# Moving the latents' transposes and the values' part of a folding from the experts' stage into attention's first unit

## The chip, the cores and the metric

The kernel runs on one core of one Trainium2 chip. The metric is the time of one execution on the device in microseconds (us); the time before is 1996.56 us, the median of three runs.

## What is computed

The reference is two layers of a transformer trunk on float32 tokens x of shape (4, 512, 512). Layer 0 adds a test-time-training attention and a ternary feed-forward network. Layer 1, with which the change deals, adds to x a latent attention and a mixture of four experts, both of the normalised x:

```
c_kv = xn @ W_DKV + b_DKV                         # 128 latent numbers per token
c_q  = xn @ W_DQ + b_DQ                           # 384
k, q = (c_kv @ W_UK + b_UK), (c_q @ W_UQ + b_UQ)  # 16 heads of 128
v    = c_kv @ W_UV + b_UV
q, k : first 64 numbers of each head replaced by rope(q @ W_QR), rope(k @ W_KR)
ctx  = softmax(q k^T / sqrt(128)) @ v             # per batch and head, 512 x 512 scores
x    = x + (ctx @ W_O + b_O) + experts(xn)
experts: token t goes to expert t % 4; silu(gate) * up, then down
```

## The kernel before

The program is one list of instructions for five engines: TensorE (PE; its weight loads are PEld), VectorE (DVE), ScalarE (ACT), GpSimd (POOL) and SyncE (SP). Every engine takes its own list in order and waits at an instruction until all that it needs is there; DMAs that SP or POOL issue stand in the same lists. A scheduler orders the lists, but instructions wrapped in `pin(...)` keep the order in which the program emits them. A tile with `bufs=1` has a single buffer: a load into it waits until the readers of its last content are done.

Layer 0 comes first and ends with the latents in memory. Two stages of layer 1 follow.

**The experts' stage** (about 1000 to 1136 us). For each expert e, `hidden(e)` computes four blocks of the gated hidden layer (products `epg` and `epu`, line L976, 128x256 each; copies `hold` on ACT, L1008 to L1014), and `returned` the way back (`epo`, L1039; for the last two experts `eox` and `eo`, L1069). Into this stage small work for attention is mixed:

- `fold` for head group 0. There are 16 heads in four head groups of four heads. Folding multiplies the up-projections of a head group by the rope's matrices (`pw`, L866: four 128x64 products each, for `uk` and three `uq`), and the values' up-projection by the rows of W_O (`pvo`, L891: one 128x512 product per head; the copy to `vo` on ACT, L892), so that attention's output comes from latents directly. `fold` is a generator; each `next` moves it one stage on: it loads a block `raw` (L883), transposes it on DVE into `wt` (L877), and multiplies. The values' part is the fifth block. It also loads one head's 128 rows of W_O into `ow` (L857), once per head, and DVE adds these rows, scaled by a bias, to `bo_part` (L895, L897). In this stage `ow` has two buffers and is loaded from SP's queue.
- for each of the four batches, four PE transposes of the latents `ckv` (`lv_tr`, L1157), and one copy on ACT to `lv` (L1158).

**The attention stage** (1136 us to the end) runs 16 units, one per head group and batch, head group outermost. A unit has four steps i, one for each 128 query rows. A step emits: the scores of four heads (`sc`, L1207, twelve products into four banks), the softmax in five slices (DVE: maximum L1225, reciprocal L1231, transpose `tt` L1236; ACT: exponential L1227, scaling L1232; then 16 DMAs `prT` on SP, L1246), between the slices a quarter of the next unit's up-projections (`pk` and `pq`, L1184; rope on DVE L1191 and L1194 and on POOL L1195, other parts on ACT L1198), one slice of the previous unit's output product (`px`, `p`, L1301), one `next` of the next head group's folding, and the context product of two steps before (`pc`, L1254, four products with `lv`; copied to `ctxT`, L1256). For each head group POOL makes four sums and differences of `vo` into `t_ops` (L1274 to L1277), which the output products read. The first unit has no output product, and its steps 0 and 1 have no context product.

In this stage `fold` is called with one buffer for `ow`, loaded from POOL's queue. Its end for each head is:

```
            pv = psum(f"pvo_{hg}_{h}")
            pin(nc.tensor.matmul(pv, lhsT=wt[:, h, :], rhs=ows[h], start=True, stop=True))
            pin(nc.scalar.copy(w["vo"][:, h, :], pv))
            ...
            if h + ow_bufs < HPG:
                output_rows(h + ow_bufs)
            if h % 2 or ow_bufs == 1:
                yield
```

and the order at the end of a step is:

```
                advance(1, outs)
                advance(1, soft)
                advance(1, folds)
                if n > 1:
                    context_of(n - 2)
```

The folding of head group hg+1 begins with the first unit of head group hg.

## Time and profile before

| | |
|---|---|
| runs | 1996.56 us median of 3 (1992.72, 1996.56, 1998.15) |
| the profiled execution's own time | 1996.04 us |
| its span in the profile | 1994.3 us |
| mean granted clock of PE | 0.994 |
| PE busy | 1938.3 us, 97% |
| DVE, ACT, POOL busy | 1169.6, 816.1, 528.2 us |
| experts' last hidden layer | 1081.6 to about 1112 us |
| attention's first unit, steps 0 to 3 | 1149.4 to 1192 us |

Times in views are us from the span's start. A float32 product is two records of PE in the timeline (twelve score products are 24 records), a PE transpose one; the end of a record is modelled, so the cost of a group is best read from its start to the start of the next. Idle time in square brackets stands in front of the instruction, with what ended it.

### The profile page before, as it was taken

How to read it: one execution, taken by the hardware profiler on the slowest of the kernel's cores; microseconds unless marked ns; L12 is line 12 of the kernel's file. 1: busy time of each engine (PE TensorE's matmuls, PEld its weight loads, DVE VectorE, ACT ScalarE, POOL GpSimd, SP SyncE). 2: the span in 40 equal slices, each digit the busy share in tenths (PEclk: the TensorE clock that was granted, in tenths of full speed). 3: DMA queues.
4: the chain of work that ended last, by engine and by line, in shares of the span. 5: the costliest groups of instructions: out<-in, count | busy, mean ns of one | idle time of the engine just before them, and what ended most of it. 6: DMA issues, size and time to landing. Idle time of an engine off the chain costs nothing.

```text
span 1994.3 us, 32414 instructions
## 1 busy us (share of the span) xinstructions
PE 1938.3 (97%) x11626; PEld 1233.3 (62%) x11626; DVE 1169.6 (59%) x2579; ACT 816.1 (41%) x1695; POOL 528.2 (26%) x643
## 2 busy tenths in 40 slices
PE   8999999999999999998999999999999999999999
PEld 6777676767766676753777744555555555555555
DVE  4445748466666657474555656556555655655565
ACT  2234333334433443422222155455545545555552
POOL 5333343424333342512000101111211121222223
PEclk9999999999999999999999999999999999999999
DMA  6757566646456455745651135444344444333344
GB/s 170 210 130 209 143 185 167 175 120 179 141 145 189 126 173 159 224 128 195 225 168 49 58 94 141 118 106 104 101 111 108 103 110 108 95 101 98 89 115 117
DMA packets 226924, 273.51 MB, mean 137 GB/s; under 512 B 88587, under 2 KB 117452, under 8 KB 226124
## 3 DMA queue, kind: packets, MB, share of 16 engines
q1 hardware_dynamic: 204928, 237.19, 43.3%
q0 software_dynamic: 9760, 28.41, 5.0%
q10 hardware_dynamic: 12076, 5.84, 1.0%
q8 instruction: 93, 1.52, 0.3%
q14 instruction: 67, 0.55, 0.1%
HBM read 174.18 MB, written 34.87 MB: 105 GB/s over the span
## 4 chain that ended last, share of the span: by engine, by line
PE 49%; DVE 1%; DMA 0%; ACT 0%; issue 0%; SPq 0%; DVEq 0%; ACTq 0%
PE pc L1254 11%; PE sc L1207 9%; PE pq L1184 8%; PE px L1301 5%; PE p L1301 4%; PE pk L1184 3%; PE epg L976 3%; PE epo L1039 1%; PE epu L976 1%; PE eox L1069 1%; PE pvo L891 1%; PE pw L866 1%; PE eo L1069 1%; DMA gu<-in_gu 0%; DVE st L1225 0%; ACT prob L1227 0%
## 5 line engine op out<-in xcount | busy, mean ns | idle before, releaser
L1225 DVE TENSOR_REDUCE st<-sc 128x1 f32<-128x512 f32 x256 | 168.9, 681 | 244.0 <-PE sc L1207 244.0
L1227 ACT ACTIVATE prob<-sc,st 128x512 f32<-128x512 f32 x256 | 175.1, 686 | 210.5 <-DVE st L1225 210.3
L1254 PE MATMUL pc<-prT,lv 128*128 128x512 f32 x512 | 230.8, 593 | 0.0
L1232 ACT ACTIVATE prob<-prob,st 128x512 f32<-128x512 f32 x256 | 181.9, 720 | 58.8 <-DVE st L1231 58.8
L1236 DVE STREAM_TRANSPOSE tt<-prob 128x512 f32<-128x512 f32 x256 | 178.4, 700 | 43.0 <-ACT prob L1232 36.5
L117 PE MATMUL pf<-xT,wg 128*128 128x256 f32 x704 | 175.6, 391 | 6.2 <-DMA wg<-in_wg 4.4
L1184 PE MATMUL pq<-cq,uq 128*128 128x512 f32 x384 | 175.2, 592 | 0.0
L117 PE MATMUL pf<-xT,wu 128*128 128x256 f32 x704 | 167.6, 381 | 1.5 <-DMA wu<-in_wu 1.5
L117 PE MATMUL pd<-wd,hid 128*128 128x512 f32 x352 | 166.1, 600 | 1.3 <-DMA wd<-in_wd 1.2
L1254 PEld LDWEIGHTS pc<-prT,lv 128*128 128x128 f32 x512 | 96.4, 190 | 100.1 <-issue 98.1
L117 PEld LDWEIGHTS pf<-xT,wg 128*128 128x128 f32 x704 | 133.2, 194 | 33.5 <-issue 4.7
L1207 PE MATMUL sc<-k,q 32*128 32x512 f32 x1024 | 145.7, 617 | 2.5 <-ACT prob L1227 2.5
L117 PEld LDWEIGHTS pf<-xT,wu 128*128 128x128 f32 x704 | 134.5, 191 | 20.5 <-DMA wu<-in_wu 1.9
L478 DVE SCALAR_TENSOR_TENSOR hid<-pf,us,sg 128x256 f32<-128x256 f32 x88 | 42.0, 478 | 156.9 <-ACT sg L477 156.4
L1184 PEld LDWEIGHTS pq<-cq,uq 128*128 128x128 f32 x384 | 74.1, 193 | 90.7 <-issue 90.0
L314 POOL TENSOR_SCALAR sk<-k,m 128x256 f32<-128x256 f32 x64 | 61.2, 968 | 179.9 <-PE pz L117 167.7
L1195 POOL TENSOR_TENSOR kr<-kr,t2k 128x512 f32<-128x512 f32 x16 | 20.3, 1270 | 332.3 <-DVE t2k L1194 332.3
L421 POOL TENSOR_SCALAR gh<-grad,m 128x256 f32<-128x256 f32 x64 | 61.2, 966 | 154.5 <-DVE grad L390 131.6
L117 PEld LDWEIGHTS pd<-wd,hid 128*128 128x128 f32 x352 | 63.4, 190 | 60.2 <-issue 43.8
L1207 PEld LDWEIGHTS sc<-k,q 32*128 32x128 f32 x1024 | 48.4, 185 | 82.7 <-issue 73.2
L477 ACT ACTIVATE sg<-pf,gs 128x256 f32<-128x256 f32 x88 | 41.6, 473 | 132.8 <-PE pf L117 132.3
L1256 ACT COPY ctxT<-pc 128x512 f32<-128x512 f32 x64 | 37.4, 585 | 127.2 <-PE pc L1254 127.1
(316 smaller groups left out, 3467.9 us busy)
## 6 DMA issues: line engine op xcount, KB each, us to landing
prT<-tt SPq DMA_DIRECT2D x992, 64.0 KB, 2.0
wd<-in_wd SPq DMA_DIRECT2D x176, 256.0 KB, 3.1
wg<-in_wg SPq DMA_DIRECT2D x88, 256.0 KB, 3.0
wu<-in_wu SPq DMA_DIRECT2D x88, 256.0 KB, 3.1
cq<-lat_d SPq DMA_DIRECT2D x48, 256.0 KB, 3.8
rows<-rows SPq DMA_DIRECT2D x128, 66.0 KB, 2.2
kv<-rows POOLq DMA_DIRECT2D x32, 264.0 KB, 4.1
gu<-in_gu SPq DMA_DIRECT2D x3, 2048.0 KB
```

The costliest lines, as they stand in the source:

```text
L117: nc.tensor.matmul(out, lhsT=lhsT, rhs=rhs, start=start, stop=stop, skip_group_check=True)
L314: nc.gpsimd.tensor_scalar_mul(sk[:, :, :, h, :], at(k1[ch], slice(0, P)), m2[:, h : h + 1])
L421: nc.gpsimd.tensor_scalar_mul(gh[:, :, h, :], g, m2[:, h : h + 1])
L976: nc.tensor.matmul(ps, lhsT=w[:, c, :], rhs=x[:, c], start=start and c == 0, stop=c == 1, skip_group_check=True)
L1184: nc.tensor.matmul(ps, lhsT=columns(ws[hg][w]), rhs=x, start=(i == 0), stop=(i == len(srcs) - 1))
L1207: nc.tensor.matmul(ps[h], lhsT=qk[f"q{c}"][r, i * P : (i + 1) * P], rhs=qk[f"k{c}"][r, :], start=(n == 0), stop=(n == 2),)
L1225: pin(nc.vector.tensor_reduce(mx, ps[h], AX.X, ALU.max, negate=True))
L1227: pin(nc.scalar.activation(pr, ps[h], AF.Exp, bias=mx, scale=1.0, accum_out=sm))
L1232: pin(nc.scalar.mul(pr, pr, sm))
L1236: nc.vector.transpose(out=tt[:, :, h - 2], in_=pr.rearrange("p (k kq j) -> p kq k j", kq=4, j=32))
L1254: pin(nc.tensor.matmul(pc, lhsT=lv[:, b, k, :], rhs=at[:, :, k, :], start=(k == 0), stop=(k == E - 1)))
L1301: nc.tensor.matmul(ps[:, q, :], lhsT=a[:, k, q * P : (q + 1) * P], rhs=w[:, k, :], start=start and k == 0 and q == 0, stop=k == 1, skip_gr ...
```

## The change

Three things are changed. `fold` takes a `part`, a slice of its five blocks, and ends early if the values' block is not in it. The experts' stage folds only the first four blocks of head group 0, and its 16 transposes of latents with their four copies are gone. In attention, a new generator `values_first` does the transposes of one batch at a time, moves the values' part of head group 0 one stage on with each, and then does the rest of that part, with one buffer for `ow` and POOL's queue. Unit 0 advances it by two in each step, where other units advance the folding by one. The folding of head group 1 begins with unit 1 instead of unit 0; the later head groups are as they were.

```diff
-    def fold(w, pool, hg, wk, psum, ow_bufs, rows=nc.sync):
+    def fold(w, pool, hg, wk, psum, ow_bufs=0, rows=nc.sync, part=slice(None)):
...
-        n = len(up_srcs)
+        n = len(folded)
         for i in range(n + 1 + ahead):
-            k = i - ahead - 1
-            if 0 <= k < n - 1:
+            k = folded[i - ahead - 1] if i > ahead else -1
+            if 0 <= k < len(ups):
...
-        wt = turned.pop(n - 1)
+        if len(ups) not in folded:
+            return
+        wt = turned.pop(len(ups))
...
-                first = fold(w0, lat, 0, wk, lambda nm: psp.tile([P, 512], F32, tag="pa", name=nm), 2)
+                first = fold(w0, lat, 0, wk, lambda nm: psp.tile([P, 512], F32, tag="pa", name=nm), part=slice(len(ups)))
...
-            if e == 2:
-                for b in range(B):
-                    pt = psp.tile([P, E, P], F32, tag="pa", name=f"lv_tr_{b}")
-                    for k in range(E):
-                        nc.tensor.transpose(pt[:, k, :], ckv[:, b, k * P : (k + 1) * P], ident)
-                    nc.scalar.copy(lv[:, b], pt)
...
+        def fold_psum(nm):
+            return ps_pj.tile([P, 512], F32, tag="pj", name=nm)
+
+        def values_first():
+
+            values = fold(w0, lat, 0, wk, fold_psum, 1, nc.gpsimd, slice(len(ups), None))
+            for b in range(B):
+                pt = ps_pj.tile([P, E, P], F32, tag="pj", name=f"lv_tr_{b}")
+                for k in range(E):
+                    pin(nc.tensor.transpose(pt[:, k, :], ckv[:, b, k * P : (k + 1) * P], ident))
+                pin(nc.scalar.copy(lv[:, b], pt))
+                next(values, None)
+                yield
+            yield from values
+
...
         for u, (hg, b) in enumerate(units):
-            if b == 0 and hg + 1 < NHG:
+            if u == 0:
+                folds = values_first()
+            if b == (hg == 0) and hg + 1 < NHG:
...
-                advance(1, folds)
+                advance(2 if u == 0 else 1, folds)
```

More of the change, by code (lines that the diff above doesn't have):

```diff
@@ L844, in group_tiles @@
         return {nm: pool.tile([P, 2, HPG * RD], F32, tag=nm, name=f"{nm}_{hg}", bufs=1) for nm in ups}
-    def fold(w, pool, hg, wk, psum, ow_bufs, rows=nc.sync):
+    def fold(w, pool, hg, wk, psum, ow_bufs=0, rows=nc.sync, part=slice(None)):
         ahead = 1
         heads = slice(hg * HPG, (hg + 1) * HPG)
-        for nm, src in zip(ups, up_srcs):
+        folded = range(len(up_srcs))[part]
+        for nm, src in list(zip(ups, up_srcs))[part]:
             nc.sync.dma_start(out=w[nm][:, 0].rearrange("p (h d) -> p h d", h=HPG), in_=src.rearrange("p (h d) -> p h d", h=H)[:, heads, :RD])
@@ L874, in fold @@
             if 0 <= i - ahead < n:
-                t = turned[i - ahead] = wk.tile([P, HPG, P], F32, tag="wt", name=f"wt_{hg}_{i - ahead}", bufs=1)
+                t = turned[folded[i - ahead]] = wk.tile([P, HPG, P], F32, tag="wt", name=f"wt_{hg}_{i - ahead}", bufs=1)
                 pin(
                     nc.vector.transpose(
-                        out=t.rearrange("p h c -> p (h c)"), in_=raws.pop(i - ahead).rearrange("p h c -> p (h c)")
+                        out=t.rearrange("p h c -> p (h c)"), in_=raws.pop(folded[i - ahead]).rearrange("p h c -> p (h c)")
                     )
@@ L881, in fold @@
             if i < n:
-                raw = raws[i] = wk.tile([P, HPG, P], F32, tag="raw", name=f"raw_{hg}_{i}", bufs=1)
-                nc.sync.dma_start(out=raw, in_=blocks_d[i][:, heads, :])
+                raw = raws[folded[i]] = wk.tile([P, HPG, P], F32, tag="raw", name=f"raw_{hg}_{i}", bufs=1)
+                nc.sync.dma_start(out=raw, in_=blocks_d[folded[i]][:, heads, :])
             if 0 <= i - n - ahead + ow_bufs - 1 < ow_bufs:
@@ L1402, in trunk_kernel @@
                     wk,
-                    lambda nm: ps_pj.tile([P, 512], F32, tag="pj", name=nm),
+                    fold_psum,
                     1,
```

## The prediction

> **What bounds the kernel now.** I read the page first, then the groups of instructions, then the order of time around the places that the change touches.

> ```profile
> PE 1938.3 (97%) x11626; PEld 1233.3 (62%) x11626; DVE 1169.6 (59%) x2579; ACT 816.1 (41%) x1695; POOL 528.2 (26%) x643
> L1157 PE MATMUL lv_tr<-ident,ckv 128*128 128x128 f32 x16 | 2.1, 277 | 0.0
> L891 PE MATMUL pvo<-ow,wt 128*128 128x512 f32 x32 | 16.0, 592 | 0.0
> ow<-in_W_O POOLq DMA_DIRECT2D x12, 256.0 KB, 3.2
> ```

> TensorE (PE) is busy for 97% of the span, so only what removes PE work or PE idleness counts. Neither moved group waits for anything (0.0 us before it). The fourth line is the price, from issue to landing, of one block of output rows on GpSimd's (POOL's) queue.

> The windows by stage say where PE has room; the columns are length, PE, PEld, DVE, ACT and POOL busy, clock, DMA share, GB/s.

> ```profile
> 1081.60:1108.40 26.80, 26.80 (x134) 21.94 (x125) 12.51 (x32) 10.89 (x25) 0.00 (x0) 1.00 0.19 61
> 1149.40:1192.00 42.60, 40.09 (x169) 17.15 (x172) 26.79 (x55) 27.31 (x58) 2.54 (x2) 0.96 0.37 98
> 1192.00:1235.00 43.00, 43.00 (x194) 21.40 (x187) 26.27 (x55) 25.45 (x57) 7.57 (x6) 1.00 0.49 129
> ```

> The last expert's hidden layer is full; unit 0 (second row) is the one attention unit with idle PE and a lower clock; unit 1 is full again, and so are the units behind it. Whatever PE gains or loses in unit 0 reaches the end undiminished. The timeline of PE shows both places.

> ```profile
> 1082.74 1.04 PE L1157 MATMUL lv_tr<-ident,ckv 128*128 128x128 f32 x8
> 1083.62 0.60 PE L976 MATMUL epg<-xe,gu 128*128 128x256 f32 x2
> ...
> 1090.62 1.88 PE L891 MATMUL pvo<-ow,wt 128*128 128x512 f32 x4
> 1092.33 1.03 PE L976 MATMUL epg<-xe,gu 128*128 128x256 f32 x4
> ...
> 1155.85 1.13 PE L1207 MATMUL sc<-k,q 32*128 32x512 f32 x4
> 1157.44 1.12 PE L1207 MATMUL sc<-k,q 32*128 32x512 f32 x2 [0.47 <-ACT prob L1227]
> 1159.35 1.21 PE L1207 MATMUL sc<-k,q 32*128 32x512 f32 x1 [0.79 <-ACT prob L1227]
> ...
> 1163.81 1.12 PE L1184 MATMUL pk<-ckv,uk 128*128 128x512 f32 x2
> ...
> 1167.44 1.13 PE L1207 MATMUL sc<-k,q 32*128 32x512 f32 x6
> 1169.84 0.69 PE L1207 MATMUL sc<-k,q 32*128 32x512 f32 x1 [1.26 <-ACT prob L1227]
> ...
> 1172.60 1.13 PE L1184 MATMUL pk<-ckv,uk 128*128 128x512 f32 x2
> ...
> 1176.15 1.00 PE L866 MATMUL pw<-W_KR,wt 128*128 128x64 f32 x8
> 1176.99 3.65 PE L1254 MATMUL pc<-prT,lv 128*128 128x512 f32 x8
> ```

> From start to start, eight transposes take 0.88 us and two pvo products 1.71. A step's twelve score products take 2.78 us undisturbed (1149.43 to 1152.21, step 0 of unit 0). Step 1's take 1163.81-1155.85 = 7.96, a loss of 5.18; step 2's take 1172.60-1167.44 = 5.16, a loss of 2.38. In both, a head's scores wait for the exponential of the step before to free their bank. In the windows of 1 us the clock is 0.69 from 1159 to 1160 and 0.50 until 1162, so the 5.18 also holds about 1.7 of half clock. Total quiet loss: 7.56 us.

> **What the change does, part by part.** In the experts' stage PE loses 16 transposes (0.88+0.95) and four pvo products (2 x 1.71): 5.25 us, in a stretch that is full, so unit 0 starts 5.25 earlier. Nothing there should begin to wait: expert 2's first product (1039.45 to 1045.49) runs without these transposes and without a wait. On SP, two loads of `ow` and `raw_4` leave the queue ahead of the experts' weights; that can only bring those weights earlier. The copies on ACT and the sums on DVE leave engines that had slack; their worth is zero. The same 5.25 us returns in unit 0, and two `pw` groups (0.84 each) leave unit 0 with head group 1's folding, to come back in units 1 and 2. PE's work is therefore unchanged, and the sum is one of idle time and clock alone. I keep the times of before, with unit 0 aligned.

> *Step 0 into 1.* Eight transposes go between the up-projection's end (1155.85) and the scores: 0.90 us of the gap is filled. The fourth head still starts at 1159.35, because its exponential sets it; their two copies on ACT come behind that exponential, at 1160.5, where ACT idled 3.29 us. Gain 0.90 if the clock falls again, and about 2.2 if not (1.3 of the 1.7 is passed on; then DVE, with one more 0.67 us transpose, is late next). PE's quiet time here was 2.84 us by pitch and went cold; step 2's 1.5 us did not; the changed gap has 1.96 if transposes keep the clock up, which lies between. I take the middle, 1.55. [...]

> *Step 1 into 2.* Eight transposes and pvo_0 (0.95+0.86) end at 1169.25; the last exponential allows the fourth head at 1169.84, by when three heads have run (0.65). The 2.38 us is filled: gain 2.38, at least 1.0 if the copies of lv and vo delay ACT.

> *Step 2: the new wait.* The fold now moves two stages per step, and in attention `ow` has one buffer (two in the experts' stage). In the built order PE has pvo_1, pvo_2 and then `pc_0`, back to back. pvo_2 needs `ow_2`, which goes into the buffer that pvo_1 and DVE's `bo_part` sum read. POOL's order is `ow_1`, the first subtraction of `t_ops<-vo`, `ow_2`, `ow_3`: so ow_2 also stands behind an instruction that waits for vo_1's copy, which on ACT comes behind all of the step's softmax. The ends:

> ```profile
> 1177.96 1.35 ACT L1232 ACTIVATE prob<-prob,st 128x512 f32<-128x512 f32 x2
> 1179.18 0.40 ACT L868 ACTIVATE uk<-pw 128x256 f32<-128x256 f32 x1
> ```

> vo_1's copy takes `uk`'s place: 1179.1 + 0.57 (median of L892) = 1179.65; handed to POOL in 0.09 (as from ctxT's copy to s_ops, 1267.58 to 1267.67) + 1.28 (t_ops) = 1181.0; issue to landing 3.2, plus 0.2 to the reader (`kv`, issued 51.1, landing 3.0 at best, is read at 54.3): 1184.4. Half of the issue instruction (0.55) is added, as the row doesn't show whether it is within the 3.2: 1184.7. pvo_1 ends at 1172.04+3.6+0.86 = 1176.5. Wait: 8.2 us. DVE's sum of ow_1 (1179.4+0.71) is done before POOL's subtraction, so POOL sets the issue. Lower end: landing 2.7, 1181.0+2.7+0.2 = 1183.9, hence 7.4; upper end: landing 4.8 and the whole issue on top, 1186.5, hence 10.0. [...]

> Behind pvo_2 on PE stand pc_0, the next scores and everything else; on DVE tt_2_3 waits behind bo_part's sum of ow_2, but its reader pc_2 comes some 20 us later. pvo_3 finds its rows (issued at about 1185.5, needed after 1196). After such a pause PE restarts cold: here it was cold for 2.9 us after restarting at 924.4 and 5.5 after 51.4, which is 1.45 to 2.75 lost at half clock; I take 2.1.

> Sum: +8.2 +2.1 -2.38 -1.55 = +6.4. Ends: 7.4+1.45-2.38-2.2 = +4.3 and 10.0+2.75-1.0-0.9 = +10.9. The profiled execution took 1996.04 us (span 1994.3, 1.7 around it), 0.5 below the median of 1996.56: 2002.4 against itself, 2002.9 against the median.

> **Rivals.** *The filling wins.* If ow_2 reached the buffer before PE comes to pvo_2 (at 1176.5, the point from which it decides), only the gains remain: 2.38 + 0.90 to 2.2, at most all 7.56. Time 1989 to 1993.3. For it speaks that ow is waited for by no product before: they stand a whole step (14 us) apart. Against it stands the single buffer and the two products side by side.
> *The same wait, at its cheap end.* The gap of step 1 stays warm, landing takes 2.7 and PE warms up at once: +4.3 to +6, 2000.9 to 2002.5, which is no measurable difference.
> *The experts' stage returns less than 5.25.* At 1022.89 a product waits 0.69 us for the copy of L1008; if the removed work hid that in expert 3's three places, +2.1 on top: about 2005. The dense second expert speaks against it.

> **How the numbers follow.** Forecast above the bound 0.58, experts' stage 0.04 (both slower), cheap end 0.30 (same), filling wins 0.08, of which 0.05 beyond 6 us. 0.3% is 6.0 us, about what a measurement of this kernel can tell from no change; runs of before lie 5.4 apart. The sum's centre is just above the bound, but its ends are lopsided upwards (2.1 below, 4.5 above), which puts most of the forecast over it. Slower 0.62, same 0.33, faster 0.05. Range: 1999.5 to 2007.3, the ends and a little of the runs' spread below; it leaves out the filling.

> **What would show it.** Right: in the changed profile PE waits 7 to 10 us once, before the third pvo, put down to the DMA of ow or to POOL; the clock falls there; the scores of step 2 show no wait; the start of unit 0 is 5 us earlier. POOL's t_ops stands just ahead of the issue. Wrong: pvo products with waits under 2 us, or a start of unit 0 that has not moved, or new waits in the last expert's first products.

## The result, and the profile after

The changed kernel took 2003.97 us (median of 7 runs, 1999.54 to 2009.12), the kernel before 1997.15 in the same comparison (7 runs, 1992.72 to 1999.32): a ratio of 1.0035, with a 95% interval of 1.0019 to 1.0051. That is 7.0 us slower by the ratio and 6.8 between the medians. The interval is clear of zero, but it lies on both sides of the 0.3% that the prediction set as its bound, so the runs do not settle on which side of the bound the change is. The profiled execution took 1999.54 us (span 1997.8, mean granted clock 0.994). That is below the median, and all that lies ahead of expert 3 ran 3.6 us quicker than in the profile of before (TensorE was at half clock there for 13.7 us instead of 20.5, which can make 3.4 us of it); so the two traces are compared from expert 3's first product to the end: before 1994.3 - 1081.78 = 912.52, after 1997.8 - 1078.15 = 919.65, which is 7.1 us more.

The page's engine line and its groups, the list of PE's waits, and the last expert's window, all of the changed kernel:

```profile
PE 1937.2 (97%) x11626; PEld 1232.2 (62%) x11626; DVE 1172.5 (59%) x2579; ACT 816.0 (41%) x1695; POOL 531.3 (27%) x647
L894 PE MATMUL pvo<-ow,wt 128*128 128x512 f32 x32 | 17.5, 629 | 7.9 <-DMA ow<-in_W_O 7.8
PE pvo L894 <- DMA ow<-in_W_O: 7.8, 1, 7.8
PE sc L1204 <- ACT prob L1224: 0.8, 1, 0.8
ow<-in_W_O POOLq DMA_DIRECT2D x16, 256.0 KB, 3.5
1078.15:1104.95 26.80, 26.80 (x123) 22.81 (x123) 14.83 (x37) 7.58 (x20) 0.54 (x1) 1.00 0.15 48
```

PE has as many instructions as before (11626) and as much busy time to 1.1 us, so the work was moved, not changed. `pvo`, which waited for nothing before, now waits once, for 7.8 us, and its mean grew from 592 to 629 ns. The scores' three waits (2.5 us together) have become one of 0.8. The last line but one says that `ow` is now loaded 16 times from POOL's queue instead of 12, at a median of 3.5 us; the last, that the last expert's hidden layer is still full. The timeline of PE shows unit 0:

```profile
1147.14 1.04 PE L1395 MATMUL lv_tr<-ident,ckv 128*128 128x128 f32 x8
1148.11 1.84 PE L1204 MATMUL sc<-k,q 32*128 32x512 f32 x6
1150.74 0.69 PE L1204 MATMUL sc<-k,q 32*128 32x512 f32 x1 [0.79 <-ACT prob L1224]
...
1153.50 1.13 PE L1181 MATMUL pk<-ckv,uk 128*128 128x512 f32 x2
...
1157.04 1.04 PE L1395 MATMUL lv_tr<-ident,ckv 128*128 128x128 f32 x8
1158.12 1.12 PE L894 MATMUL pvo<-ow,wt 128*128 128x512 f32 x2
1159.17 1.47 PE L1204 MATMUL sc<-k,q 32*128 32x512 f32 x8
...
1162.29 1.13 PE L1181 MATMUL pk<-ckv,uk 128*128 128x512 f32 x2
...
1165.84 1.02 PE L894 MATMUL pvo<-ow,wt 128*128 128x512 f32 x2
1174.69 2.04 PE L894 MATMUL pvo<-ow,wt 128*128 128x512 f32 x2 [7.83 <-DMA ow<-in_W_O]
1176.53 5.64 PE L1251 MATMUL pc<-prT,lv 128*128 128x512 f32 x8
1182.10 1.14 PE L1204 MATMUL sc<-k,q 32*128 32x512 f32 x8
...
1188.43 1.02 PE L894 MATMUL pvo<-ow,wt 128*128 128x512 f32 x2
```

The transposes stand in both gaps as predicted, and the scores behind them lose less. pvo_1 and pvo_2 stand side by side, and between them PE is idle from 1166.70 (1165.84 + 0.86) to 1174.69, 7.99 us. pvo_2 and pc_0 then take 7.41 us instead of 4.44. pvo_3, a step later, waits for nothing. The timelines of ACT, POOL and DVE show what pvo_2's rows waited for:

```profile
1169.03 0.60 ACT L895 COPY vo<-pvo 128x512 f32<-128x512 f32 x1
1169.21 0.71 DVE L900 SCALAR_TENSOR_TENSOR bo_part<-ow,b_UV,bo_part 128x512 f32<-128x512 f32 x1
1169.71 1.33 POOL L1271 TENSOR_TENSOR t_ops<-vo 128x512 f32<-128x512 f32 x1 [7.41 <-ACT vo L895]
1170.99 0.55 POOL L858 DMA_DIRECT2D ow<-in_W_O  x1
1174.64 0.75 DVE L900 SCALAR_TENSOR_TENSOR bo_part<-ow,b_UV,bo_part 128x512 f32<-128x512 f32 x1 [4.72 <-DMA ow<-in_W_O]
```

pvo_1's copy on ACT comes 2.3 us after the product, behind the step's softmax; POOL's subtraction waits for it; the request stands behind the subtraction on POOL; and 3.65 us after the request DVE and PE read the rows.

### The profile page after: what moved, and what is told of

Same layout as the page of the kernel before. It is cut to its first block, busy times and chain, and to the rows that moved or that the text cites. A ratio compares the mean times of both kernels' runs of the same rounds, so it can differ in the third digit from the quotient of the medians.

```text
span 1997.8 us, 32413 instructions
## 1 busy us (share of the span) xinstructions
PE 1937.2 (97%) x11626; PEld 1232.2 (62%) x11626; DVE 1172.5 (59%) x2579; ACT 816.0 (41%) x1695; POOL 531.3 (27%) x647
## 4 chain that ended last, share of the span: by engine, by line
PE 50%; ACT 1%; DVE 0%; DMA 0%; issue 0%; POOL 0%; DVEq 0%; POOLq 0%; ACTq 0%
PE pc L1251 11%; PE sc L1204 9%; PE pq L1181 8%; PE px L1298 5%; PE p L1298 4%; PE epg L979 3%; PE pk L1181 3%; PE epu L979 1%; PE epo L1042 1%; PE pvo L894 1%; PE eox L1072 1%; PE pw L867 1%; PE eo L1072 1%; ACT prob L1224 0%; DMA ow<-in_W_O 0%; DVE st L1222 0%
## 6 DMA issues: line engine op xcount, KB each, us to landing
wd<-in_wd SPq DMA_DIRECT2D x176, 256.0 KB, 3.1
wg<-in_wg SPq DMA_DIRECT2D x88, 256.0 KB, 3.0
wu<-in_wu SPq DMA_DIRECT2D x88, 256.0 KB, 3.2
cq<-lat_d SPq DMA_DIRECT2D x48, 256.0 KB, 4.0
```

## The experiments

Theory R: the loss is the reload of the single buffer between two products that stand side by side, with the half clock behind it; the moved work itself gains in unit 0's gaps. Theory M: the moved work costs more in unit 0 than in the experts' stage, with or without that wait. Theory C: the moved copies on ACT delay the softmax. Ratios are to the kernel before in the same comparison (its medians were 1997.89 us for e1 to e4 and 1997.39 for e5 to e8), with 95% intervals. Differences in us are worked out from the ratios; those between medians lie up to 2.3 us away from them.

**Memory of its own for each head's rows (e1).** The blocks of heads 1 to 3 go into tiles that lie idle in unit 0 and are requested at once; PE's order is that of the changed kernel.

```diff
         def output_rows(h):
-            ows[h] = wk.tile([P, HS], F32, tag="ow", name=f"ow_{hg}_{h}", bufs=ow_bufs)
+            if own and h:
+                ows[h] = own[h - 1]
+            else:
+                ows[h] = wk.tile([P, HS], F32, tag="ow", name=f"ow_{hg}_{h}", bufs=ow_bufs)
...
+            idle = [s_ops[:, k].rearrange("p c x -> p (c x)") for k in range(3)]
-            values = fold(w0, lat, 0, wk, fold_psum, 1, nc.gpsimd, slice(len(ups), None))
+            values = fold(w0, lat, 0, wk, fold_psum, 1, nc.gpsimd, slice(len(ups), None), idle)
```

> The changed kernel with one edit: in unit 0 the rows of heads 1 to 3 are loaded into three blocks of s_ops, which stands idle there, so no load waits for a product; PE's order stays as in the changed kernel. Theory R (the reload: the single buffer of ow makes pvo_2 wait, and the pause makes the clock fall): the wait of 8.0 us and the 3.0 us of half clock go, the filled gaps stay (2.6 and 1.7 us), so 4 us less than before: 1993, 11 less than the changed kernel. Rival M (the moved work itself: it was hidden in the experts' stage, or head group 1's later folding delays something, and the wait only took up slack): 2001 to 2005, with the loss showing as waits elsewhere behind unit 0. Rival C (the copies lv and vo on ACT lengthen the softmax): waits of the scores in steps 2 and 3, about before's 1997.

Measured: 1994.42 us, ratio 0.9977 (0.9966 to 0.9988). PE's timeline there:

```profile
1153.06 1.13 PE L1210 MATMUL sc<-k,q 32*128 32x512 f32 x1 [0.79 <-ACT prob L1230]
...
1169.86 1.88 PE L900 MATMUL pvo<-s_ops,wt 128*128 128x512 f32 x4
1171.58 3.60 PE L1257 MATMUL pc<-prT,lv 128*128 128x512 f32 x8
```

pvo_1 and pvo_2 run back to back and pc_0 follows at full speed. Each taken against the kernel before, this is 0.0035 + 0.0023 = 0.0058 of the time under the changed kernel, 11.6 us, and it is also 4.6 us faster than the kernel before (3.5 between the medians). Only where the rows lie and when they are requested differs, so the whole loss and more is the reload's, with the half clock behind it; theories M and C are out as causes of the loss.

**One stage per step (e2).** The single buffer stays; unit 0 advances by two in its first two steps only, so no two products stand together, and head group 1's folding follows when the first is done.

```diff
-                folds = fold(
...
+                folds = chain(
+                    folds,
+                    fold(ws[hg + 1], pool, hg + 1, wk, fold_psum, 1, nc.gpsimd),
                 )
...
-                advance(2 if u == 0 else 1, folds)
+                advance(2 if u == 0 and i < 2 else 1, folds)
```

> The changed kernel with the single buffer kept, but from step 2 on the folding moves one stage per step, so that the products pvo_1, pvo_2 and pvo_3 stand a step apart (pvo_3 in unit 1, head group 1's folding one step later). Theory R: each load has some 10 us instead of none, needs about 5.5 (sum on DVE, 0.55, 3.6 to landing), so no wait; 1993, the same as with buffers of their own. Rival M: 2001 to 2005 as the moved work is the same. If a single buffer were too slow even with a step between, waits of 1 to 3 us before each pvo and 1996 to 2000.

Measured: 1995.62 us, ratio 0.9985 (0.9972 to 0.9998). No product of `pvo` waits; a context product waits 1.1 us for `prT` in unit 1. So it isn't the single buffer alone that costs, but two of its readers in a row.

**The transposes alone (e3).** The kernel before, with the 16 transposes and four copies moved to unit 0 and nothing else.

```diff
-            if e == 2:
-                for b in range(B):
-                    pt = psp.tile([P, E, P], F32, tag="pa", name=f"lv_tr_{b}")
...
+        turning = latents_turned()
...
+                advance(2, turning)
                 advance(1, folds)
```

> The kernel before with one part of the change: only the 16 transposes of latents and their copies move into unit 0's steps 0 and 1; the values' part stays in the experts' stage and head group 1 folds from unit 0. Theory R: no wait arises, the first gap gives 0.9 (clock falls) to 2.6 us (clock stays), the second about 1: 2 to 3.5 us less than before, 1993.5 to 1995. Rival M: at best no difference, 1997; if transposes count for nothing with the clock, the gap of step 1 stays cold and the gain is 1.9 at most.

Measured: 1995.04 us, ratio 0.9979 (0.9967 to 0.9991): this half of the change gains, 4.2 us (1.8 to 6.6 by the interval).

**The values' part alone (e4).** The changed kernel with the transposes left in the experts' stage.

```diff
             values = fold(w0, lat, 0, wk, fold_psum, 1, nc.gpsimd, slice(len(ups), None))
             for b in range(B):
-                pt = ps_pj.tile([P, E, P], F32, tag="pj", name=f"lv_tr_{b}")
-                for k in range(E):
-                    pin(nc.tensor.transpose(pt[:, k, :], ckv[:, b, k * P : (k + 1) * P], ident))
-                pin(nc.scalar.copy(lv[:, b], pt))
                 next(values, None)
                 yield
```

> The changed kernel with the transposes back in the experts' stage: only the values' part moves. Theory R: the wait of 8 us and 2 to 3 us of half clock are there in full, the first gap is unfilled as before (loss 5.2, or 3.5 if it stays warm) and the second gives about 0.9: 8 to 10 us more than before, 2005 to 2007, slower than the changed kernel by 1 to 3.5. Rival M with the cost in the transposes: about before, 1997.

Measured: 2006.58 us, ratio 1.0038 (1.0023 to 1.0053), 7.6 us. Its timeline has the same wait:

```profile
1180.93 2.05 PE L894 MATMUL pvo<-ow,wt 128*128 128x512 f32 x2 [8.13 <-DMA ow<-in_W_O]
```

The loss is in this half. The two halves, -4.2 and +7.6, add up to +3.4, and the whole is at +7.0; with intervals of about 2.4 and 3.0 to each side that is no contradiction and no proof of additivity. That e4 is slower than the changed kernel, as was expected, the ratios (1.0038 and 1.0035) do not show.

**Rows from ACT's queue (e5).** The changed kernel with `nc.scalar` in place of `nc.gpsimd` for the rows.

```diff
-            values = fold(w0, lat, 0, wk, fold_psum, 1, nc.gpsimd, slice(len(ups), None))
+            values = fold(w0, lat, 0, wk, fold_psum, 1, nc.scalar, slice(len(ups), None))
```

> The changed kernel with one argument different: the output rows of the values' folding are requested from ScalarE's queue instead of GpSimd's. The single buffer, the order on TensorE and all arithmetic stay. In the changed kernel the third block was requested 1.36 us after vo_1's copy had ended (1169.63 to 1170.99), because GpSimd's subtraction of t_ops stood in front; on ScalarE the request follows vo_1's copy at once. Theory R (the price is the reload of the single buffer): the wait before pvo_2 stays but falls from 7.8 to about 6.5 us (6.0 to 7.0), the half clock behind it stays at 2 to 3 us, and the time is 1 to 2 us under the changed kernel's, 2001.5 to 2003. Rival (the order of GpSimd's queue is the whole of it): the wait goes to below 2 us and the time to the 1995 of the kernels without the wait. Rival (the rows wait for bandwidth and not for their request): the wait stays at 7.5 to 8 us.

Measured: 2000.85 us, ratio 1.0020 (1.0006 to 1.0035). The wait fell less than expected; the timelines of ACT, DVE and PE:

```profile
1171.59 0.60 ACT L895 COPY vo<-pvo 128x512 f32<-128x512 f32 x1
1173.00 0.35 ACTq L858 DMA_DIRECT2D ow<-in_W_O  x1
1171.78 0.71 DVE L900 SCALAR_TENSOR_TENSOR bo_part<-ow,b_UV,bo_part 128x512 f32<-128x512 f32 x1
1176.49 0.75 DVE L900 SCALAR_TENSOR_TENSOR bo_part<-ow,b_UV,bo_part 128x512 f32<-128x512 f32 x1 [4.01 <-DMA ow<-in_W_O]
1176.53 2.04 PE L894 MATMUL pvo<-ow,wt 128*128 128x512 f32 x2 [7.11 <-DMA ow<-in_W_O]
```

The request now starts 0.51 us after the other reader of the buffer, DVE's sum, has ended (1172.49), and 0.81 after vo_1's copy. The trace names nothing that released this request; in e7, below, it names that sum, and the request starts 0.54 us after it. So DVE's sum is probably what is late next, once POOL's subtraction is gone. By pitch (from start to start) the wait is 1176.53 - 1169.26 = 7.27 instead of 7.99. Of the 0.72 us, 0.55 is the earlier request (3.74 us after pvo_1's end instead of 4.29), the rest a quicker landing: the order of POOL's queue was worth about 0.6 us of the wait, not 1.4. The time is 3 us under the changed kernel's by the ratios, but their intervals overlap.

**Head group 1's folding later (e6).** The kernel before with one condition changed.

```diff
-            if b == 0 and hg + 1 < NHG:
+            if b == (hg == 0) and hg + 1 < NHG:
```

> The kernel before with one edit: the folding of head group 1 starts with unit 1 instead of unit 0, as it does in the changed kernel; nothing else is moved. Theory R holds that this part costs nothing and brings nothing, since TensorE's work is the same and the two moved groups of pw stand in full stretches afterwards: within 1.5 us of the kernel before, ratio 0.999 to 1.001, no new wait above 1 us. Rival: the later folding is itself part of the 2 to 3 us that the kernels without the long wait gained over the kernel before (DVE and ScalarE relieved in unit 0's tight steps): 2 us faster. Rival on the other side: the folding ends too late for head group 1's first projection: 2 us or more slower.

Measured: 1998.20 us, ratio 1.0015 (0.9999 to 1.0030). By the interval a gain of more than 0.2 us is excluded; a loss of up to 6 us is not. The profile shows one new wait, 1.3 us of a context product for `prT` in unit 1. So the later start is not where e1 and e2 found their time (e3 does not have it).

**The wait alone (e7).** The kernel before, advancing head group 1's folding by two stages in one step of unit 2. Nothing leaves the experts' stage.

```diff
-                advance(1, folds)
+                advance(2 if (u, i) == (2, 0) else 1, folds)
```

> The kernel before with one edit: in step 0 of unit 2 the folding of head group 1 is advanced by two stages instead of one, so that its products pvo_1 and pvo_2 stand together although ow has one buffer; its last stages come one step earlier. Nothing leaves the experts' stage. It makes the disputed wait without the move. Theory R: TensorE waits before pvo_2 of head group 1 for the rows: the sum of bo_part that reads the buffer, the request and the landing put the wait at about 5.4 us (4.5 to 7), the clock falls to 0.50 behind it and costs 2 to 3 us more, and nothing gives that back, as TensorE is full there: 7 to 9.5 us slower than the kernel before, ratio 1.0035 to 1.0048. Rival (a pause of TensorE in a unit is partly made up later, by waits that then fall away): a wait of the same length, but 0 to 4 us slower.

Measured: 2005.70 us, ratio 1.0043 (1.0028 to 1.0058), 8.6 us slower. Timelines of POOL, DVE and PE:

```profile
1248.11 0.71 DVE L897 SCALAR_TENSOR_TENSOR bo_part<-ow,b_UV,bo_part 128x512 f32<-128x512 f32 x1
1249.36 0.54 POOL L857 DMA_DIRECT2D ow<-in_W_O  x1 [13.61 <-DVE bo_part L897]
1246.61 1.02 PE L891 MATMUL pvo<-ow,wt 128*128 128x512 f32 x2
1252.31 2.05 PE L891 MATMUL pvo<-ow,wt 128*128 128x512 f32 x2 [4.68 <-DMA ow<-in_W_O]
1254.15 4.85 PE L1254 MATMUL pc<-prT,lv 128*128 128x512 f32 x8
```

The wait is 4.84 us by pitch (1247.47 to 1252.31) and the slow restart another 2.2, together 7.0 of the 8.6 (5.6 to 11.6 by the interval). One argument makes the loss, in another unit and for another head group, and nothing later gives it back.

**Spread otherwise (e8).** As e1, with pvo_0 in step 0, pvo_1 in step 1, and one product in each of steps 2 and 3. The result of pvo_0 goes to a bank of another pool, which the lines below leave out.

```diff
+            values = fold(w0, lat, 0, wk, bank, 1, nc.gpsimd, slice(len(ups), None), idle)
+            advance(3, values)
+            yield
             for b in range(B):
...
-                next(values, None)
+                if b % 2:
+                    next(values, None)
...
-                advance(2 if u == 0 else 1, folds)
+                advance(2 if u == 0 and i < 2 else 1, folds)
```

> The kernel with heads 1 to 3's rows in memory of their own, with the moved work spread otherwise over unit 0: pvo_0 stands in step 0 behind the eight transposes, pvo_1 in step 1, pvo_2 in step 2 and pvo_3 in step 3, one each. Theory: the rest of quiet time between steps 0 and 1 (2.6 us lost in the changed kernel) shrinks by pvo_0's 0.86 us, to 1.5 to 1.9, and step 1 to 2 keeps 0.7 to 1.5; so 0 to 1.5 us faster than that kernel's 1994.4, 1993 to 1994.5. If what sets the fourth head's scores is DVE's and ScalarE's softmax and vo's copy stands in front of an exponential, the gap only moves: 1994.5 to 1996.

Measured: 1991.72 us against 1997.39 for the kernel before, ratio 0.9983 (0.9967 to 0.9999). That is under both ranges that were expected. The wait between steps 0 and 1 shrank from 0.79 to 0.64, and a context product waits 1.5 us for `prT` in unit 1. The interval overlaps those of e1 to e3: all four beat both kernels, and which of them is best stays open.

**The clock's marks (e9 to e12).** With windows of 1 us, the times at which the granted clock falls and rises were read from every profile up to 1984 us, and all lie on a grid of 3.41 us that has another phase in each execution. In the kernel before the clock is at half five times: from 50.06 and 265.10 for 6.82 us each, from 159.28, 923.86 and 1159.38 for 3.42 each. Behind the first fall, the others come 109.22, 215.04, 873.80 and 1109.32 us later, which is 32, 63, 256 and 325 times 3.413 us. 62 such stretches were read in the 14 profiles, and each begins and ends on its profile's grid to 0.03 us. Windows of that grid, for the changed kernel (length, PE, PEld, DVE, ACT and POOL busy, clock, DMA share, GB/s):

```profile
1149.92:1153.33 3.41, 2.62 (x19) 1.09 (x18) 2.80 (x7) 2.94 (x6) 0.00 (x0) 1.00 0.00 0
1153.33:1156.75 3.42, 3.42 (x9) 1.57 (x9) 3.17 (x7) 2.69 (x7) 1.18 (x1) 1.00 0.53 153
...
1166.99:1170.40 3.41, 0.00 (x0) 0.00 (x0) 2.22 (x6) 2.64 (x6) 0.69 (x1) 1.00 0.44 106
1170.40:1173.81 3.41, 0.00 (x0) 0.00 (x0) 0.00 (x0) 0.00 (x0) 1.13 (x2) 0.50 0.63 159
1173.81:1177.23 3.42, 2.54 (x3) 1.17 (x4) 1.37 (x2) 0.46 (x1) 0.20 (x1) 0.50 0.19 50
1177.23:1180.64 3.41, 3.41 (x5) 1.33 (x4) 0.00 (x0) 0.12 (x1) 0.34 (x1) 0.50 0.66 169
1180.64:1184.05 3.41, 3.41 (x24) 1.44 (x26) 0.00 (x0) 0.59 (x1) 0.00 (x0) 1.00 0.40 98
```

In these rows the clock of each window goes with the work of the one before: behind the empty one from 1166.99 it is 0.50, behind the one with 2.54 us of work (74%) it is still 0.50, behind the first full one 1.00. Busy time alone is not the measure, though: far ahead of attention, at 262.45 to 265.87, the same trace has a window with 1.62 us of other products behind which the clock stays at 1.00. What else counts stays open. The slow restart here lasts from 1174.69 to 1180.64, 5.95 us. Two kernels were profiled twice more, unchanged, for other phases.

> The changed kernel once more, unchanged, for another profiled execution. In the profiles so far every change of TensorE's clock lies on a grid of 3.41 us that has another phase in each execution: the stretches at half clock are 3.4, 6.8 or 10.2 us long, to within 0.05. Theory G (the clock is set at the marks of that grid, by what TensorE did in the 3.41 us before): the wait before pvo_2 is 8.0 us by pitch again (7.8 to 8.2), but the time at half clock after pvo_2's start is any value from 2.9 to 6.3 us by the phase, so that pvo_2 and pc_0 lose 1.4 to 3.2 us, not 2.97 each time; the whole stretch at half clock is 6.8 or 10.2 us. Rival F (warming up takes a fixed time of work): half clock ends 5.9 us after pvo_2's start again, within 0.2.

> As the run before it, for a third phase. Theory G: again the wait of 8.0 us, and another time at half clock behind it than in the other two executions. Rival F: 5.9 us again.

> The kernel with heads 1 to 3's rows in memory of their own once more, unchanged. In its first profile the gap between steps 0 and 1 went to half clock, in the changed kernel's, with the same instructions there, it did not. Theory G: it falls or not by the phase. Where one window of the grid holds the wait of 0.8 us and the transposes, it falls (there the products without the transposes filled 1.89 of 3.41 us); where the transposes lie in the window before, it stays (2.62 of 3.41). The fourth head's scores take 4.5 us from their start to the next projection in the one case, 2.8 in the other. Rival F (this program's order sets it): it falls again, at the same place.

> As the run before it, for a third phase of the same kernel. Theory G: half clock in the gap only if the window of the grid that holds the wait has under about 2.2 us of products, transposes left out. Rival F: half clock at the same place again.

One time each was taken: 2007.61 and 2003.90 us for the changed kernel, 1988.28 and 1994.36 for e1's, beside 2001.27 for the kernel before. Measured in the traces, for the changed kernel: waits of 7.68 and 8.27 us by pitch (1175.22 to 1182.90, and 1170.96 to 1179.23), just outside the 7.8 to 8.2 that was expected; half clock for 10.24 us in both, until 5.64 and 5.53 us after pvo_2's start. The rival of a fixed time asks for 5.9 within 0.2, so these two are outside, but near. All six waits of `pvo` together decide: PE restarts 0.88 us behind a mark of its grid in the changed kernel's first profile, 1.18 in e9, 1.29 in e10, 2.14 in e4, 2.48 in e7 and 2.93 in e5, and two windows (6.83) less that give the measured 5.95, 5.64, 5.53, 4.7, 4.35 and 3.9 us of half clock after the restart. So a fixed time is out, and the spread comes with where in a window PE restarts. In the gap of steps 0 to 1 the changed kernel fell to half clock in e9 and stayed in e10; e1's kernel fell in its first profile and stayed in e11 and e12. So the rival that the program's order sets it is out: one program does both. The windows that hold the gap, of e9 (fell) and e11 (stayed), each with the window after it:

```profile
1154.41:1157.82 3.41, 2.62 (x16) 1.20 (x18) 3.13 (x8) 2.69 (x7) 0.00 (x0) 1.00 0.00 0
1157.82:1161.23 3.41, 3.41 (x17) 1.43 (x14) 1.95 (x4) 1.87 (x4) 0.00 (x0) 0.50 0.14 40
```

```profile
1149.38:1152.79 3.41, 2.62 (x19) 1.09 (x18) 2.80 (x8) 2.96 (x6) 0.00 (x0) 1.00 0.00 0
1152.79:1156.20 3.41, 3.41 (x8) 1.44 (x8) 3.16 (x8) 2.55 (x6) 1.04 (x1) 1.00 0.57 153
```

Both are busy for 2.62 us; in e9's 0.59 of it are transposes, in e11's none. The fall costs 1.7 us: the fourth head's scores take 1162.03 - 1157.56 = 4.47 us to the next projection in e9, 2.76 in the changed kernel's first profile. The clock also explains much of the spread between executions of one kernel: e11 and e12 are 6.1 us apart, their profiles hold 10.2 and 23.9 us at half clock, all ahead of attention, and half of the difference is 6.8.

## Why the prediction held

The forecast was 2002.9 us and 6.4 us over the kernel before; measured were 2003.97 and 7.0. Its terms, in the order of its sum:

- *The wait*, 8.2: 7.99, 7.68 and 8.27 in three executions. The chain was the one written down: ACT's copy behind the softmax, POOL's subtraction, the request, the landing. From request to reader it took 3.65 where 3.7 was assumed (3.2, 0.2 and half of the request's 0.55). That POOL sets the request is right, but by little: e5 gives 0.55 us as its lead over the next reader, DVE's sum.
- *The slow restart*, 2.1, with bounds of 1.45 and 2.75: pvo_2 lost 0.98 and pc_0 1.99, 2.97 together, above the upper bound, so this term was mis-sized. The prediction took the 2.9 and 5.5 us of two restarts as two prices; they are two positions on the grid, and the position is a matter of the execution. The other executions lost 1.95 (e5) to 2.8 (e9).
- *Step 0 into 1*, a gain of 1.55 (0.9 cold, with the clock falling to 0.50 in the gap; 2.2 warm, with the clock at 1.00): the loss fell from 5.18 to 1153.50 - 1148.11 - 2.78 = 2.61, a gain of 2.57, warm. Cold, as in e9, it is 1.7 less: 0.9. The cold case was right and the warm one 0.4 short; the mean between them happens in none of these executions. (Step 2's quiet time, put at 1.5 us there, is 1169.84 - 1167.44 - 0.66 = 1.74 by the reckoning that gives step 1's 2.84.)
- *Step 1 into 2*, 2.38: the scores take 1162.29 - 1159.17 = 3.12 and 0.3 more is lost around the transposes, in all 0.66 instead of 2.38, a gain of 1.72.
- *The experts' stage*, 5.25: from expert 3's first product to unit 0's first projection 53.82 us before (1081.78 to 1135.60) and 48.84 after (1078.15 to 1126.99), 4.98. The rival of a smaller return fails but for 0.27.

Together 7.99 + 2.97 - 2.57 - 1.72 + 0.27 = 6.9, against the 7.1 of the two traces. The mechanism was right; that the total came so near is partly luck. Against the forecast the restart is 0.87 us more, the second gap 0.66 and the experts' stage 0.27, the first gap 1.02 less and the wait 0.21 less, and these nearly cancel. An execution with the first gap cold, such as e9's, has 1.7 us more.

The rival "the filling wins" named its own condition, rows there when PE comes to pvo_2. e1 makes that condition true, with 1994.42 us: the gain is real, some 4.6 us, and the wait and its restart take 11 us away from it.

The prediction left it as an "if" whether transposes keep the clock up, and e3's rival asked what follows if they count for nothing. The runs speak against the latter for these float32 transposes. A window with 2.16 us of work, score products alone, stands right ahead of a window at half clock (the kernel before, both windows):

```profile
1155.97:1159.38 3.41, 2.16 (x10) 0.50 (x10) 3.24 (x9) 2.69 (x7) 0.00 (x0) 1.00 0.00 0
1159.38:1162.80 3.42, 3.42 (x16) 1.54 (x17) 1.44 (x3) 1.14 (x2) 0.00 (x0) 0.50 0.08 19
```

In e5 a window had only 1.77 us of scores and 1.03 of transposes, and the clock stayed at 1.00 (e2's, 1149.04 to 1152.45, likewise, with 1.91 and 1.04):

```profile
1149.71:1153.12 3.41, 2.80 (x15) 1.38 (x13) 3.40 (x8) 2.69 (x7) 0.00 (x0) 1.00 0.00 0
1153.12:1156.53 3.41, 3.23 (x19) 1.39 (x20) 2.81 (x6) 2.44 (x7) 0.00 (x0) 1.00 0.05 12
```

So here they counted, if perhaps for less than their time: of the windows with 2.62 us of work, those of score products alone kept the clock at 1.00 (the changed kernel, e11), and behind e9's, with 0.59 of transposes in it, it was 0.50.

## What to carry to other kernels

Before work is moved into a gap, list what each moved product reads and how many buffers that has: a single buffer was free here while its readers stood a step apart, and cost sum, request and landing as soon as two stood side by side on an engine that was otherwise full (4.8 us, and 7.3 to 8.3 where the softmax and a copy on ACT came first). Such a pause was paid a second time in the slow restart, with 1.95 (e5) to 2.97 us (the changed kernel), so count the wait and 2 to 3 us. When a move has a good and a bad half, do the halves alone: here the transposes gained 4 us and the values' part lost 8, and spreading the products over steps kept the gain.
